# The 7x7 offset convolution of a deformable layer: from even and odd columns to even and odd rows and columns, with its weights read from DRAM piece by piece

## The chip, the core and the metric

The kernel runs on one core of a Trainium2 chip. A core has a matrix engine (TensorE, PE in the profile), three engines for elementwise work (VectorE, called DVE; ScalarE, called ACT; GpSimd, called POOL), a sync engine (SP) that here only issues DMAs, an on-chip memory with 128 partitions (SBUF), and an accumulator memory that the matrix engine writes (PSUM). The engines run independent instruction streams, each in its own order, and wait for each other by semaphores. The metric is the device time of one launch in microseconds (us), less is better. The kernel takes 9018.82 us (median of three runs, 9018.04 to 9021.72). The profiled execution took 9017.3 us, of which 9015.5 us are the span from its first to its last instruction.

## What is computed

The input is 8 samples of 384 channels of 32x32 pixels in float32. Four residual layers follow each other, each on a group-normalised input. The change touches the second, the deformable layer. It splits the channels into three groups of 128 with kernel sizes 3, 5 and 7, and for each group does this:

```python
def deform_block(x, ow, ob, dw, pw, pb, K):
    pad = K // 2
    offsets = conv2d(x, ow, ob, pad)          # 128 channels -> 2*K*K
    out = deform_depthwise(x, offsets, dw, K, pad)
    return conv2d(out, pw, pb, 0)

c3, c5, c7 = jnp.split(x, 3, axis=1)
out = jnp.concatenate([deform_block(c3, ..., 3), deform_block(c5, ..., 5), deform_block(c7, ..., 7)], axis=1)
return out * se_weight(out, fc1_w, fc2_w)
```

`deform_depthwise` samples the input bilinearly at K*K shifted positions per pixel, weighs each by the channel's depthwise weight and sums. The change is about `conv2d(x, ow, ob, 3)` for K = 7: 128 input channels, 98 output channels, 49 taps.

## The kernel before

The deformable layer is `deform_fast`. For each sample it handles the groups g = 0, 1, 2 (K = 3, 5, 7). The taps of a group are gathered into octets of eight taps that share the partitions, and one octet of a single tap; an octet is split into four parts (two for the single tap). One part of one octet is a **unit**. A sample has 6 + 14 + 26 = 46 units, numbered through all samples; `first[b, g]` is the first unit of group g of sample b, and t0 stands below for `first[b, 0]`.

In each unit VectorE makes weighted input cells (`fxk`, `weigh`, line 1640) and products of two hat functions (`fsm`, `product`, line 1657), and TensorE multiplies them into five PSUM banks (`wacc`, `products`, line 1694: 32 recorded instructions, 8 for a part of the single tap, two for each float32 matmul). The hats come from ScalarE (`hats_x`, lines 1600 and 1605, into `fhx`; `hats_y`, lines 1617 and 1622, into `fhy`), two buffers each, made from sampling positions (`fpyx`) that a DMA reads back from DRAM and spreads over the partitions.

The order of work on PE, DVE and ACT is written out by hand (`tc.manual_schedule`): a loop over unit numbers u, here called **slots**. In slot u the code emits, in this order: the load of positions due (`loads`), what was put in places act0, pe0 and dve0 of the slot, TensorE's products of unit u alternating with VectorE's work for unit u + 1, the hats due, and places act1, dve1 and pe1. `put(slot, place, fn)` fills the places. SP's order is not written out; its queue takes the DMAs of all these steps.

The three offset convolutions of sample b are spread through the slots of the sample before. The 3x3 one (`conv`, line 1317) is put whole at t0 - 13, the 5x5 one in six pieces at t0 - 12 to t0 - 7. The 7x7 one (`fir`, line 1279) is put in 14 pieces at t0 to t0 + 13. All use one PSUM bank (tag "conv", one buffer).

The 7x7 convolution already uses a trick along x: even and odd output columns share work. `fir_sum` (line 1265, at t0 - 1) adds even and odd columns of the input into `xs`; three accumulations (parts) over half-width images with 3, 4 and 4 combined column weights replace two with seven each. With seven rows these are 77 matmuls for 98 outputs, each over up to 512 positions (32 rows by 16 columns). `fir_take` evacuates a part: ScalarE for the shared sum (line 1288), VectorE adding it for the even and the odd columns (line 1293). The 11 combined columns of each of the seven rows are made once by `fir_weights` (DMAs on ACT's queue, six subtractions on POOL, line 1196) and stay in SBUF as `fow7`: 77 x 98 floats, 30.2 KB in each partition. `fir_end` then checks the range, adds the grid and writes the positions to DRAM at t0 + 14.

When a group's last unit is done, `sums_act` (ScalarE, line 1396) copies part of `wacc` and `sums` (VectorE, line 1401) adds the rest, both at the first slot of the next group; TensorE cannot start the next group before both are done, since `wacc` has one buffer.

Of the kernel before, what the change touches and what calls it, by code (L numbers as in the profile page):

```python
# [60 lines left out]
    ((0, 1), (-1, 0), (1, 2)),  # L61
    ((0, 6), (-2, 3), (-1, 7), (1, 9)),
    ((0, 5), (-1, 10), (1, 8), (2, 4)),
)
HXN, HYN, SMN = 1856, 1792, 832
# [34 lines left out]
class Net:  # L100
# [956 lines left out]
    def deform_fast(self, src, dst):  # L1057
        tc, nc, ins = self.tc, self.nc, self.ins
        with ExitStack() as ctx:
            wp = ctx.enter_context(tc.tile_pool(name="w1f", bufs=1))  # L1060
            self.q1 = ctx.enter_context(tc.tile_pool(name="q1", bufs=1))
            self.q2 = ctx.enter_context(tc.tile_pool(name="q2", bufs=2))
            self.mm = ctx.enter_context(tc.tile_pool(name="mm1", bufs=2, space=PSUM))
            self.win_acc = ctx.enter_context(tc.tile_pool(name="win_acc", bufs=1, space=PSUM))

            self.xn0 = self.q1.tile([P, G, L], F32, name="fxn")
            nc.sync.dma_start(out=self.xn0, in_=src(0))
            self.f = {}
            for g, K in enumerate(KS):
# [3 lines left out]
                ow = wp.tile([P, K * NFIR if n == 1 else K2, rows if n == 1 else st], F32, name=f"fow{K}")  # L1073
# [5 lines left out]
                if n == 1:  # L1079
                    self.fir_weights(ow, ins[f"ow{K}"])  # L1080
                else:
                    queue.dma_start(out=ow[:, :, :rows], in_=ins[f"ow{K}"])
# [44 lines left out]
            for u, (b, g, j, h) in enumerate(units):  # L1127
                if h == 0:
                    one = self.parts(g, j) == 2
                    loads[u - (4 if one else 5)] = b, g, j  # L1130
                    for t, fn, k in (
                        ((-2, self.hats_x, 0), (-2, self.hats_y, 0), (-1, self.hats_y, 1))
                        if one
                        else ((-3, self.hats_x, 0), (-2, self.hats_y, 0), (-1, self.hats_y, 1), (0, self.hats_x, 1))
                    ):
                        hats.setdefault(u + t, []).append((fn, b, g, j, k))
# [12 lines left out]
            with tc.manual_schedule(engines=engines):  # L1149
                for u in range(min(slots), max(slots) + 1):  # L1150
# [16 lines left out]
                    for fn, *args in sorted(hats.get(u, ()), key=lambda h: h[0] == self.hats_y):  # L1167
# [21 lines left out]
    def fir_weights(self, ow, src):  # L1189
        nc = self.nc  # L1190
        w = ow.rearrange("p (y k) o -> p y k o", k=NFIR)
        v = src.rearrange("p (y x) o -> p y x o", x=7)
        for k, x in enumerate((1, 3, 5, 0, 6, 2, 4)):
            nc.scalar.dma_start(out=w[:, :, k, :], in_=v[:, :, x, :])
        for d, i, j in ((7, 5, 0), (8, 6, 2), (9, 4, 2), (10, 3, 0), (5, 5, 1), (6, 6, 1)):
            nc.gpsimd.tensor_tensor(w[:, :, d, :], w[:, :, i, :], w[:, :, j, :], ALU.subtract)


    def block_steps(self, b, g, first, put, weights, src, dst):
# [62 lines left out]
        def fir_sum():  # L1262
            xs = s["xs"] = self.q1.tile([P, H, W // 2], F32, name="fxs", tag="fxs")
            x4 = xg().rearrange("p (h i e) -> p h i e", e=2, i=W // 2)
            nc.vector.tensor_tensor(xs, x4[:, :, :, 0], x4[:, :, :, 1], ALU.add)


        def fir(part, t0, t1):
            if t0 == 0:
                s["ps"] = self.mm.tile([P, HL], F32, name="ps_off", tag="conv", bufs=1)  # L1270
            x4 = xg().rearrange("p (h i e) -> p h i e", e=2, i=W // 2)
            x3 = (s["xs"], x4[:, :, :, 1], x4[:, :, :, 0])[part]
            o = s["ps"][:used].rearrange("p (h i) -> p h i", i=W // 2)
            work = [(dy, d, k) for dy in (0, -3, -2, -1, 1, 2, 3) for d, k in FIR[part]]
            for t in range(t0, t1):
                dy, d, k = work[t]
                ya, yb = max(0, -dy), min(H, H - dy)
                xa, xb = max(0, -d), min(W // 2, W // 2 - d)
                nc.tensor.matmul(  # L1279
                    o[:, ya:yb, xa:xb], ow[:, (dy + pad) * NFIR + k, :],  # L1280
                    x3[:, ya + dy : yb + dy, xa + d : xb + d], start=(t == 0), stop=(t == len(work) - 1),
                )

        def fir_take(part):
            ps = s["ps"][:used]
            if part == 0:
                s["fs"] = self.q1.tile([P, HL], F32, name="ffs", tag="fxs")
                nc.scalar.activation(s["fs"][:used], ps, AF.Identity, bias=ob[:used])
                return
            if part == 1:  # L1290
                s["pos"] = self.q1.tile([P, cols], F32, name="fpos", tag="fpos")
            pos = s["pos"][:used].rearrange("p (i e) -> p i e", e=2)[:, :, part - 1]
            nc.vector.tensor_tensor(pos, ps, s["fs"][:used], ALU.add)
# [170 lines left out]

        if g == 0:
            t = s0 - self.units_of(G - 1)
# [11 lines left out]
            put(t + 13, "pe1", conv, 0, 0, K2)  # L1478
            put(t + 14, "dve0", offsets, 0)
        elif g == 1:  # L1480
            t = first[b, 0] - 12
            for i in range(6):
                put(t + i, "pe1", conv, 0, K2 * i // 6, K2 * (i + 1) // 6)
            put(t + 6, "dve0", offsets, 0)
        else:
            t = first[b, 0]
            put(t - 1, "dve1", fir_sum)
            k = 0
            for part, pieces in enumerate((4, 5, 5)):
                nw = K * len(FIR[part])  # L1490
                for i in range(pieces):
                    where = "pe0" if t + k in (first[b, 0], first[b, 1]) else "pe1"
                    put(t + k, where, fir, part, nw * i // pieces, nw * (i + 1) // pieces)
                    k += 1
                put(t + k, "dve0" if part else "act0", fir_take, part)
# [130 lines left out]
    def unit_dve(self, b, g, j, part):  # L1626
# [9 lines left out]
        def weigh(k):  # L1636
            t = self.q2.tile([P, 8, P], F32, name="fxk", tag="fxk", bufs=3)
# [399 lines left out]
```

## Time and profile before

| | |
|---|---|
| median of three runs | 9018.82 us |
| profiled execution, whole | 9017.3 us |
| its span | 9015.5 us |
| busy PE / DVE / ACT / POOL over the span | 7552.9 / 7509.5 / 5808.8 / 5548.2 us |
| mean granted TensorE clock | 0.911 of full |
| first wacc matmul of samples 3 and 4 | 3855.5 and 4179.7 us |
| matmuls of line 1279, recorded instructions | 1232 |
| matmuls of line 1317, recorded instructions | 1376 |
| matmuls of line 1694, recorded instructions | 10624 |

Busy times are unions of an engine's instructions. The profile records two PE instructions for each float32 matmul (1232 is 8 samples x 77 x 2), with overlapping durations, so that only the union or the distance between starts says what a matmul costs. The deformable layer lies between about 2795 us (its first DMAs) and 5450 us; in the forty slices of the busy table these are slices 13 to 24, where POOL is idle. After its start one sample follows the other every 324.2 us. The numbers for a stretch of time are read from the busy times by windows, those for a line from its group of instructions in a window.

### The profile page before, as it was taken

To read this page: it belongs to the slowest core of one execution; us is meant where nothing else is said; L and a number is where in the kernel's file an instruction comes from. 1 tells how busy PE (TensorE), PEld (TensorE's weight loads), DVE (VectorE), ACT (ScalarE), POOL (GpSimd) and SP (SyncE) were. 2 spreads that over 40 slices of the span, in tenths; PEclk is the share of its full clock that TensorE was granted. 3 is DMA by queue.
4 is the path that set the end of the run, shared out by engine and by line. 5 is a ranking of instruction groups with operands and counts; after the bars stand their busy time and mean duration, and the time that the engine had idled before them with its cause. 6 is when DMAs were issued, how large, how long until landed. Compare 5 with 4: busy or idle time off the path is not lost. (4 is left out here: it accounts for less than half of the span.)

```text
span 9015.5 us, 90034 instructions
## 1 busy us (share of the span) xinstructions
PE 7552.9 (84%) x29176; PEld 3742.1 (42%) x29176; DVE 7509.5 (83%) x8421; ACT 5808.8 (64%) x9437; POOL 5548.2 (62%) x3362
## 2 busy tenths in 40 slices
PE   7888888888886999989899895688888888888876
PEld 2232232232223767767766772233333333333333
DVE  6999999999994878877877885888888989888872
ACT  6777777777773555555655564676767777776740
POOL 6999999999993000000000003898998989899954
PEclk8899899899887999999999997899998999899988
DMA  4545545545544253253443433466666656666646
GB/s 128 124 122 123 124 122 123 124 122 122 124 120 111 73 129 93 78 131 93 102 107 102 109 90 99 121 148 150 150 155 160 147 145 147 154 147 153 159 140 114
DMA packets 786426, 1122.96 MB, mean 125 GB/s; under 512 B 269266, under 2 KB 420978, under 8 KB 752152
## 3 DMA queue, kind: packets, MB, share of 16 engines
q1 hardware_dynamic: 724548, 1107.05, 50.1%
q10 hardware_dynamic: 61396, 10.06, 0.7%
q8 instruction: 232, 3.80, 0.2%
q14 instruction: 250, 2.05, 0.1%
HBM read 933.97 MB, written 182.91 MB: 124 GB/s over the span
## 5 line engine op out<-in xcount | busy, mean ns | idle before, releaser
L531 POOL TENSOR_TENSOR db<-dub,bc 128x1024 f32<-128x1024 f32 x1536 | 3605.4, 2356 | 372.1 <-DVE hs L543 171.4
L523 ACT ACTIVATE da<-dtb,vec 128x512 f32<-128x512 f32 x3072 | 2122.4, 691 | 604.0 <-DVE hs L556 404.8
L543 DVE TENSOR_TENSOR_SCAN da<-da,db 128x1024 f32<-128x1024 f32 x960 | 2193.2, 2285 | 128.1 <-ACT da L523 89.0
L464 POOL TENSOR_TENSOR dt<-dt,sp_e 128x512 f32<-128x512 f32 x96 | 122.4, 1275 | 2715.5 <-DMA bc<-bcd 2711.3
L1694 PE MATMUL wacc<-fsm,fxk 128*128 128x195 f32 (+21 forms) x10624 | 1584.2, 306 | 190.0 <-DVE fsm L1657 88.7
L1694 PEld LDWEIGHTS wacc<-fsm,fxk 128*128 128x128 f32 x10624 | 1469.9, 194 | 366.6 <-DVE fsm L1657 180.6
L543 DVE TENSOR_TENSOR_SCAN hs<-da,db 128x1024 f32<-128x1024 f32 x576 | 1315.3, 2283 | 195.7 <-POOL db L516 80.6
L554 POOL TENSOR_TENSOR hs<-hs,bc 128x1024 f32<-128x1024 f32 x576 | 1356.8, 2356 | 33.2 <-ACT st L549 33.2
L1657 DVE TENSOR_TENSOR fsm<-fhy,fhx 128x143 f32<-128x143 f32 (+40 forms) x3280 | 1088.4, 396 | 295.3 <-PE wacc L1694 283.3
L556 DVE TENSOR_TENSOR hs<-da,bc 128x1024 f32<-128x1024 f32 x960 | 1175.6, 1225 | 124.6 <-PE y L566 75.5
L566 PE MATMUL y<-hs,cols 128*32 128x512 f32 x6144 | 971.3, 644 | 290.8 <-POOL hs L554 267.2
L1640 DVE TENSOR_TENSOR fxk<-fxt,fwk 128x1024 f32<-128x1024 f32 (+1 forms) x688 | 814.3, 1184 | 35.1 <-PE wacc L1694 28.3
L1617 ACT ACTIVATE fhy<-fpyx,cell 128x416 f32<-128x416 f32 (+10 forms) x832 | 422.8, 580 | 523.6 <-DVE fsm L1657 523.2
L566 PEld LDWEIGHTS y<-hs,cols 128*32 128x32 f32 x6144 | 190.1, 113 | 1006.3 <-issue 484.1
L643 PE MATMUL ps_m<-hid,wm 128*128 128x512 f32 x1152 | 550.7, 633 | 62.0 <-ACT hid L638 27.9
L1600 ACT ACTIVATE fhx<-fpyx,cell 128x416 f32<-128x416 f32 (+10 forms) x664 | 372.0, 629 | 347.8 <-DVE fsm L1657 347.8
L624 PE MATMUL ps_h<-t,wm 128*128 128x512 f32 x1152 | 529.4, 603 | 42.4 <-DVE sp_e L456 26.0
L356 PE MATMUL ps_in<-xn,winr 128*128 128x512 f32 x576 | 328.1, 716 | 173.9 <-ACT xn L345 125.6
L643 PEld LDWEIGHTS ps_m<-hid,wm 128*128 128x128 f32 x1152 | 226.7, 202 | 395.2 <-issue 282.3
L1279 PE MATMUL ps_off<-fxn,fow 128*98 128x465 f32 (+10 forms) x896 | 385.8, 579 | 0.0
L624 PEld LDWEIGHTS ps_h<-t,wm 128*128 128x128 f32 x1152 | 215.4, 192 | 361.3 <-issue 272.9
L575 PE MATMUL ps_z<-xn,winr 128*128 128x512 f32 x576 | 303.0, 674 | 47.7 <-DVE sp_e L456 47.7
(215 smaller groups left out, 9675.8 us busy)
## 6 DMA issues: line engine op xcount, KB each, us to landing
dtb<-dtd SPq DMA_DIRECT2D x768, 256.0 KB
dub<-dtd SPq DMA_DIRECT2D x768, 256.0 KB
fpyx<-fposd SPq DMA_DIRECT2D x104, 1024.0 KB
fxt<-fxd SPq DMA_DIRECT2D x96, 1024.0 KB
wm<-in_w SPq DMA_DIRECT2D x96, 768.0 KB
bc<-bcd SPq DMA_DIRECT2D x256, 256.0 KB
x<-x SPq DMA_DIRECT2D x71, 768.0 KB
dtd<-dt SPq DMA_DIRECT2D x192, 256.0 KB
```

The lines of the kernel that those rows point to most:

```text
L523: nc.scalar.activation(da[:, i, :], s["dtb", j][:, k, :], AF.Exp, scale=na[:, j, n + i : n + i + 1])
L531: nc.gpsimd.tensor_tensor(db, du, s["bc"][p][:, 0], ALU.mult)
L543: nc.vector.tensor_tensor_scan(h1, da1, db1, 0.0, ALU.mult, ALU.add)
L554: nc.gpsimd.tensor_tensor(s["hs", m], s["hs", m], c, ALU.mult)
L556: nc.vector.tensor_tensor(hs_tile(s, m), s["da", m], c, ALU.mult)
L566: nc.tensor.matmul(s["y"][k * IP : (k + 1) * IP, :], sel, s["hs", p * NSUB + k][:, i, :], start=mlp and p == 0 and i == 0, stop=p == NQP - ...
L624: nc.tensor.matmul(ps, s["w1", q][:, k, f * P : (f + 1) * P], s["t"][:, k, :], start=(k == 0), stop=(k == G - 1))
L643: nc.tensor.matmul(ps, s["w2", q][:, f, o * P : (o + 1) * P], s["hid", q][:, f, :], start=(f == 0), stop=(f == 3))
L1617: nc.scalar.activation(hy[:, at : at + (yb - ya) * W], s["pyx", j][:, 0, ya * W : yb * W], AF.Abs, bias=bias)
L1640: nc.vector.tensor_tensor(t[:, :n], x, wk[:, j : j + 1, :].to_broadcast([P, n, P]), ALU.mult)
L1657: nc.vector.tensor_tensor(self.sub(sm, at, [(r * w, n), (w, r), (1, w)]), self.sub(hy, hy_at[by] + xa, [(r * W, n), (W, r), (1, w)]), self ...
L1694: nc.tensor.matmul(a[:, ya - 4 * o : yb - 4 * o, xa:xb], k, self.sub(sm, sm_at[by], [(w, yb - ya), (1, w)]), start=o not in s["open"], sto ...
```

## The change

The 7x7 convolution is split along y in the same way as along x. Its input becomes nine images of 16 x 16: sums and single phases of rows times sums and single phases of columns. The 11 x 11 = 121 combined weights serve 121 matmuls of up to 256 positions. They are worked out in five accumulations (`FIR_PH`), two blocks of them side by side in the PSUM bank in four of the five, and in 3 + 2 + 3 + 4 + 4 = 16 pieces (`FIR_PC`).

The combined weights no longer stay in SBUF. `fir_weights` makes them once in a temporary pool (47.4 KB per partition), with nine loads on ACT's queue, 18 subtractions on POOL and nine stores on ACT's queue to a DRAM tile `fwd` (121 x 98 x 128 floats, 6.07 MB). The temporary pool is closed before the pool `q2` is opened, so that the tiles of `q2` take its place. In each sample every piece loads its own six to eight weights into one of four buffers, three slots ahead.

The pieces move: 3x3 from one piece at t0 - 13 to three at t0 - 17 to t0 - 15; 5x5 from six at t0 - 12 on to nine at t0 - 14 to t0 - 6; 7x7 from 14 at t0 on to 16 at t0 - 5 to t0 + 10, with `fir_sum` at t0 - 6 and `fir_end` at t0 + 11. The load and the normalisation of a sample's input move four slots ahead, from t0 - 25 to t0 - 14 to t0 - 29 to t0 - 18. The positions of a single-tap octet are loaded five slots ahead instead of four and its `hats_x` made three slots ahead instead of two; in a slot with both kinds of hats, `hats_y` comes first. `fxk` has four buffers instead of three, `fsm` seven instead of five.

```diff
+FIR = (((0, 0), (-1, 1), (1, 2)), ((0, 3), (-2, 4), (-1, 5), (1, 6)), ((0, 7), (-1, 8), (1, 9), (2, 10)))
+FIR_PH = (((0, 0), (0, 1)), ((0, 2),), ((1, 0), (2, 0)), ((1, 1), (2, 1)), ((1, 2), (2, 2)))
+FIR_PC = (3, 2, 3, 4, 4)
...
+            self.fwd = self.dram.tile([P, NFIR * NFIR, 2 * 49], F32, name="fwd", bufs=1)
+            with tc.tile_pool(name="fw", bufs=1) as fw:
+                self.fir_weights(fw.tile([P, NFIR, NFIR, 2 * 49], F32, name="firw"), ins["owf"])
             self.q2 = ctx.enter_context(tc.tile_pool(name="q2", bufs=2))
...
-                    loads[u - (4 if one else 5)] = b, g, j
+                    loads[u - 5] = b, g, j
...
-                        ((-2, self.hats_x, 0), (-2, self.hats_y, 0), (-1, self.hats_y, 1))
+                        ((-3, self.hats_x, 0), (-2, self.hats_y, 0), (-1, self.hats_y, 1))
...
-                    for fn, *args in sorted(hats.get(u, ()), key=lambda h: h[0] == self.hats_y):
+                    for fn, *args in sorted(hats.get(u, ()), key=lambda h: h[0] == self.hats_x):
...
-        for k, x in enumerate((1, 3, 5, 0, 6, 2, 4)):
-            nc.scalar.dma_start(out=w[:, :, k, :], in_=v[:, :, x, :])
-        for d, i, j in ((7, 5, 0), (8, 6, 2), (9, 4, 2), (10, 3, 0), (5, 5, 1), (6, 6, 1)):
-            nc.gpsimd.tensor_tensor(w[:, :, d, :], w[:, :, i, :], w[:, :, j, :], ALU.subtract)
+        at = ((slice(0, 5), slice(0, 5)), (slice(7, 8), slice(5, 6)), (slice(10, 11), slice(6, 7)))
+        for y, ys in at:
+            for x, xs in at:
+                nc.scalar.dma_start(out=w[:, y, x, :], in_=src[:, ys, xs, :])
+        diffs = ((5, 7, 1), (7, 7, 0), (9, 3, 2), (3, 3, 0), (6, 10, 2), (8, 4, 1))
+        for d, i, j in diffs:
+            for y in (slice(0, 5), slice(7, 11, 3)):
+                nc.gpsimd.tensor_tensor(w[:, y, d, :], w[:, y, i, :], w[:, y, j, :], ALU.subtract)
+        for d, i, j in diffs:
+            nc.gpsimd.tensor_tensor(w[:, d], w[:, i], w[:, j], ALU.subtract)
...
+            nc.scalar.dma_start(out=o, in_=w[:, r0:r1, c0:c1, :].rearrange("p r c o -> p r (c o)"))
...
         def fir_sum():
...
+            nc.vector.tensor_tensor(xs, x[:, :, :, 0], x[:, :, :, 1], ALU.add)
...
+            nc.vector.tensor_tensor(xr, x[:, :, 0], x[:, :, 1], ALU.add)
...
+            nc.vector.tensor_tensor(xss, xr[:, :, 0::2], xr[:, :, 1::2], ALU.add)
...
+        def fir_load(i):
+            k, _, piece = pieces[i]
+            t = s["fw", i] = self.q2.tile([P, FIR_W, used], F32, name="fw", tag="fw", bufs=4)
+            nc.sync.dma_start(out=t[:, : len(piece)], in_=self.fwd[:, k : k + len(piece)])
...
+                nc.tensor.matmul(
+                    o[:, ya:yb, xa:xb], s["fw", i][:, k, :],
+                    fir_src(r, c)[:, ya + dy : yb + dy, xa + dx : xb + dx], start=start, stop=stop,
+                )
...
-            put(t + 13, "pe1", conv, 0, 0, K2)
-            put(t + 14, "dve0", offsets, 0)
+            for i in range(3):
+                put(t0 - 17 + i, "pe1", conv, 0, 3 * i, 3 * i + 3)
+            put(t0 - 14, "dve0", offsets, 0)
...
+            for i in range(9):
+                put(t0 - 14 + i, "pe1", conv, 0, K2 * i // 9, K2 * (i + 1) // 9)
+            put(t0 - 5, "dve0", offsets, 0)
...
+            put(t0 - 6, "dve1", fir_sum)
+            t = t0 - 5
             k = 0
-            for part, pieces in enumerate((4, 5, 5)):
...
+            for ph, n_pc in enumerate(FIR_PC):
+                for _ in range(n_pc):
+                    put(t + k - 3, "dve0", fir_load, k)
+                    put(t + k, "pe0" if t + k in (t0, first[b, 1]) else "pe1", fir, k)
                     k += 1
-                put(t + k, "dve0" if part else "act0", fir_take, part)
+                put(t + k, "dve0" if ph > 1 else "act0", fir_take, ph)
             put(t + k, "dve0", fir_end)
...
-            t = self.q2.tile([P, 8, P], F32, name="fxk", tag="fxk", bufs=3)
+            t = self.q2.tile([P, 8, P], F32, name="fxk", tag="fxk", bufs=4)
...
-            sm = self.q2.tile([P, SMN], F32, name="fsm", tag="fsm", bufs=5)
+            sm = self.q2.tile([P, SMN], F32, name="fsm", tag="fsm", bufs=7)
```

The new `fir_take` evacuates five accumulations. The first two (ScalarE, three copies of 256 values) go to `fs`; the third is combined with them by three VectorE additions of 2 x 256 values; the fourth and the fifth each take two VectorE additions of 256 values into `fpos`. Four of these takes must be done before the next accumulation's first piece may start, since the PSUM bank has one buffer.

## The prediction

> **What bounds the kernel.** I read the page's busy slices first, to see where the layer lies and which engine is full there, then one sample by stretches, then the groups of the convolution's line, then the timeline at the one long gap. The layer is slices 13 to 24:
>
> ```profile
> PE   7888888888886999989899895688888888888876
> DVE  6999999999994878877877885888888989888872
> ```
>
> TensorE is at eight or nine tenths and VectorE at seven or eight. A period (324.2 us, sample 3 to 4) by stretches; columns are the stretch, its length, busy time (and count) of PE, weight loads, DVE, ACT and POOL, clock, DMA share, GB/s:
>
> ```profile
> 3848.87:3964.18 115.31, 112.84 (x535) 71.35 (x535) 73.03 (x159) 63.68 (x98) 0.00 (x0) 1.00 0.47 121
> 3964.18:3993.73 29.55, 26.14 (x185) 24.98 (x183) 29.25 (x62) 13.84 (x19) 0.00 (x0) 0.88 0.55 148
> 3993.73:4005.43 11.70, 2.04 (x17) 1.94 (x17) 5.23 (x14) 10.65 (x18) 0.00 (x0) 0.80 1.01 258
> 4005.43:4085.00 79.57, 71.64 (x431) 64.47 (x431) 77.17 (x166) 51.91 (x71) 0.00 (x0) 0.94 0.30 71
> 4085.00:4139.10 54.10, 54.10 (x376) 39.90 (x374) 41.21 (x92) 30.33 (x40) 0.00 (x0) 1.00 0.14 41
> 4139.10:4173.06 33.96, 30.84 (x202) 28.46 (x201) 33.59 (x70) 16.20 (x25) 0.00 (x0) 1.00 0.51 120
> ```
>
> The first stretch holds the 7x7 convolution (slots t0 to t0 + 13), the fifth the 3x3 and 5x5 ones: there TensorE has no gap and VectorE idles. In the second, fourth and sixth no convolution runs and VectorE is full. The third is a gap: K = 5 ends, K = 7 begins, and PE waits 9.65 us behind ScalarE's hats and copies. So **a matmul saved counts only in stretches one and five**, and matmuls moved to stretch six count in full, as its PE slack is 3 us. The convolution:
>
> ```profile
> L1279 PE MATMUL ps_off<-fxn,fow 128*98 128x480 f32 (+10 forms) x112 | 48.2, 579 | 0.0
> L1279 PE MATMUL ps_off<-fxs,fow 128*98 128x480 f32 (+6 forms) x43 | 17.7, 557 | 2.6 <-DVE fxs L1265 2.6
> ```
>
> `fxs` is read with adjacent elements, `fxn` with every second. The mean tile is 464.4 positions for `fxs` (30.29 rows after clipping by 15.33 columns) and 454.3 for `fxn` (30.29 by 15). Busy time per instruction, 17.7 / 43 = 412 ns and 48.2 / 112 = 430 ns, gives **0.886 ns and 0.947 ns a position**.
>
> **Matmuls, step by step.** Before: 21 contiguous and 56 stride-2 matmuls of two instructions, 42 x 0.412 + 112 x 0.430 = 65.5 us a sample. After: clipped sums over the nine images give 7,636 contiguous positions (33 matmuls) and 19,920 stride-2 ones (88), against 9,752 and 25,440. Cost 2 x (7,636 x 0.886 + 19,920 x 0.947) = 51.3 us. **Saved: 14.2 us of TensorE a sample.** Two bounds on the price. Smaller tiles: the wacc group's instructions (L1694) take 198.7 / 1328 = 150 ns on tiles of 143 positions in the mean, 1.04 ns a position with all small ones in it; that is the upper end for the new mean of 228 (57.3 us), and the lower end is the old price. Strided rows: [...] by the row stride-2 costs 7% more and it is 51.3. I take the row. New images also skip every second line of rows, which no row shows: if that doubles the stride's surcharge, 2 x 19,920 x 0.061 = 2.4 us is lost[...].
>
> **By stretch after the change**, at 51.3 / 121 = 0.424 us a matmul:
> - Stretch six gains pieces 0 to 4 (33 matmuls, 14.0 us) and becomes TensorE's: 30.84 + 14.0 = 44.8 us (before 33.96).
> - Group boundary at t0. Before, PE waited 1.3 + 2.47 us. Now piece 5 opens accumulation three at the head of the slot and needs the take of accumulation two, behind ScalarE's hats and `sums_act`. In the trace these end at 3853.2; TensorE would be free at 3847.5 + 3.2 = 3850.7. With the 0.4 us copy the wait is 2.9 us, VectorE's `sums` beside piece 5.
> - Slots t0 to t0 + 10: PE's work outside the convolution in stretch one is 112.84 - 65.1 = 47.7, of which slots t0 + 11 to t0 + 13 hold 11.8. So 35.9 + 88 x 0.424 = 73.2. ScalarE has 12.5 us of work at the K = 3 to 5 boundary where PE will have 9.7: plus 3.
> - Slots t0 + 11 to t0 + 13 lose their pieces and fall to VectorE: 15.2 us of its work there (before 25.4).
> - Stretches two to four: 120.8 us. Two more `fsm` buffers let VectorE enter them two products ahead (0.6 + 0.6 us each with its share of `fxk`): minus 2.5. At the gap, `hats_y` first changes nothing: `sums_act` still waits for both hats, which start at VectorE's last product (3994.54).
> - Convolutions 3x3 and 5x5: 54.1 us as before; spreading them over slots t0 - 17 to t0 - 6 (4060.6 to 4143.6) uses PE's slack there, 2.0 of 83.0 us: minus 1.5.
>
> Sum 44.8 + 2.9 + 76.2 + 15.2 + 118.3 + 52.6 = 310.0, saving 14.2 a sample. That it equals the matmul saving is chance: more waits appear, some go.
>
> **Other engines.** VectorE gains 1.1 us in `fir_sum` (0.7 + 0.7 + 0.4 for 0.7) and 2.4 in the takes (three of 0.69, four of about 0.42 by the 0.40 us products, for two of 0.69), most of it where it idles 42 us; without that cover it would cost 3.5 a sample. ScalarE's 0.7 us more is inside its waits.
>
> **DMA.** Each sample adds 16 loads and 6.07 MB on SP's queue, 27 us at the 225 GB/s seen when the DMAs are full. From 3830 to 3900 they are 0.86 busy (211 GB/s): cells and positions, 1 MB each, 4.6 us. Slots t0 - 5 to t0 + 8 hold 16 MB; with 4.9 MB more that is 93 us of transfer in about 103. So it fits, barely. A load is issued three slots ahead (some 20 us) and waits in SP's order for the buffer of four pieces before, freed one slot earlier; behind it wait positions and cells. [...] by the row, cells go out as buffers free (3837.6, 3838.3, 3839.4, 3844.9), and the fourth overlaps less. [...] I take **1 us**. Saving 13.2 x 8 samples = 106 us.
>
> **Start of the layer, once.** ACT's queue gets 11 more DMAs at 0.55 us, before the normalisation's square that waited for that queue until 2833.9: 6 us. POOL subtracts 23.5 us (six each of 490, 196 and 1,078 values at 1,524 ns per 686, for 9.1): from 2808.3 to 2832, so the stores do not wait much longer than ACT would. They take 28 us to about 2865, where the DMAs are 0.27 busy, and hold the memory under `q2`; the first positions, needed at 2873.8, come after. Piece 0 follows the 5x5 convolution (end 2867.7 + 6). Ends -5 and +30; I take **+6**.
>
> **Forecast**: 9017.3 - 106 + 6 = **8917 us**; against the median, 1.5 above the profiled execution, it would be 8919, a difference that the range swallows. Its own range is 8885 to 8945.
>
> **Rivals.**
> - *Half is lost* to waits in the shorter stretch one (ScalarE at each boundary, five takes on one bank instead of three, DMA at 90%): 6 us a sample more, 8965. For it: ScalarE's 12.5 us at the boundary, the full DMAs. Against: VectorE is further ahead there.
> - *Balance closes stalls too*: VectorE waited 36.2 us a sample for PE in `fsm`, and PE 10.3 for VectorE. If the deeper buffers remove half the 10 us gap and 4 of those 10.3, 8 x 9 more goes: 8845. Against: the gap is ScalarE's.
> - *Slower*: the weights come late. Loads of eight pieces (t0 - 1 to t0 + 6) sit behind the cells; if each stops TensorE for half a 1 MB transfer, 2.3 us, that is 18.4 a sample against 14.2 saved: 9017.3 + 34 + 6 = 9057. It decides from 0.9 us a piece (14.2 / 16). For it: DMAs at 1.0 in two runs of ten us there. Against: three slots of lead.
>
> Chances: forecast 0.52, half lost 0.22, balance 0.19, slower 0.07. 0.2% is 18 us, about what a measurement of this kernel can tell from no change: faster by that 0.92, within it 0.03 (the tail of the half-lost case), slower 0.05. The range for eight in ten runs from 8840 to 8970.
>
> **What would show it.** The convolution's group at about 51 us a sample, 0.42 us a matmul, stride-2 tiles dearer; the period at 310; PE without gaps from t0 - 5 to t0 + 10 but 3 us at t0 and t0 + 6; slots t0 + 11 on with VectorE full; the gap before K = 7 still near 10 us; few or no PE waits ended by a DMA of the piece weights. It would be wrong if those waits are there by the dozen, or if the first wacc matmul comes later than 2920.

## The result and the profile after

The changed kernel takes **8857.13 us** (median of four runs, 8852.23 to 8860.34) against 9018.67 us before: ratio 0.982, 95% interval 0.9803 to 0.9837. It is 161.5 us faster; 8917 us was forecast. The profiled execution took 8859.41 us, its span is 8857.3 us.

The busy tenths, in 40 equal slices of the span:

```profile
PE   7888888888884899999999975788888888888886
DVE  6999999999995788988898886888898988888872
```

The layer lies in slices 13 to 24 as before. After worse slices 13 and 14 (4 and 8 for 6 and 9) TensorE stands at nine tenths up to slice 23, where before it fell to eight three times, and VectorE fills up too. The gain is in the steady part of the layer and its start is dearer.

For both kernels I cut one sample's period at the slots at which groups and convolutions begin: slots 0 to 10 from t0, 11 to 19, 20 to 28, 29 to 40, 41 to 45. Busy time by these windows, before (columns as in the forecast: stretch, its length, busy time and count of PE, weight loads, DVE, ACT and POOL, clock, DMA share, GB/s):

```profile
3855.52:3938.80 83.28, 83.28 (x394) 52.82 (x395) 55.62 (x121) 46.88 (x73) 0.00 (x0) 1.00 0.53 138
3938.80:4005.43 66.63, 53.57 (x332) 43.88 (x330) 49.68 (x110) 34.71 (x52) 0.00 (x0) 0.91 0.47 127
4005.43:4060.61 55.18, 49.24 (x280) 42.97 (x281) 52.78 (x111) 33.53 (x44) 0.00 (x0) 0.92 0.35 83
4060.61:4143.64 83.03, 81.04 (x559) 65.92 (x557) 69.92 (x155) 48.91 (x67) 0.00 (x0) 1.00 0.16 42
4143.64:4179.71 36.07, 30.48 (x180) 25.49 (x179) 31.47 (x67) 22.58 (x36) 0.00 (x0) 1.00 0.65 147
```

and after:

```profile
3813.64:3884.16 70.52, 70.52 (x445) 60.80 (x445) 52.28 (x117) 46.70 (x72) 0.00 (x0) 1.00 0.82 211
3884.16:3941.84 57.68, 42.22 (x298) 40.39 (x297) 53.28 (x119) 33.61 (x50) 0.00 (x0) 0.85 0.57 161
3941.84:3990.66 48.82, 46.05 (x280) 40.50 (x280) 48.79 (x106) 35.64 (x51) 0.00 (x0) 0.97 0.38 83
3990.66:4072.62 81.96, 81.92 (x557) 64.29 (x557) 74.05 (x161) 51.75 (x69) 0.00 (x0) 1.00 0.15 40
4072.62:4113.61 40.99, 40.53 (x251) 36.95 (x251) 32.35 (x67) 19.62 (x33) 0.00 (x0) 1.00 0.80 193
```

A period falls from 324.2 to 300.0 us, 24.2 a sample. TensorE's busy time falls by 16.4 (297.6 to 281.2), its idle time by 7.9 (26.6 to 18.7), and VectorE's idle time from 64.7 to 39.2 at the same work. The first two stretches lose 12.8 and 9.0 us, the third 6.4 although it holds no convolution in either kernel, the fourth 1.1; the last, which takes pieces in (17.8 us of 7x7 matmuls for 4.2), grows by only 4.9. TensorE is now full in the first, fourth and fifth, and VectorE in the third.

The groups of the period after (line, engine, operation, tiles, count, busy us and mean ns, idle before and what ended it):

```profile
L1759 PE MATMUL wacc<-fsm,fxk 128*128 128x143 f32 (+31 forms) x1328 | 196.0, 306 | 18.3 <-ACT fhy L1682 9.7 <-DVE fsm L1722 8.3
L1722 DVE TENSOR_TENSOR fsm<-fhy,fhx 128x132 f32<-128x132 f32 (+35 forms) x410 | 135.4, 399 | 7.3 <-PE wacc L1759 7.2
L1320 PE MATMUL ps_off<-fxn,fw 128*98 128x210 f32 (+5 forms) x128 | 27.3, 366 | 0.0
L1320 PE MATMUL ps_off<-fxq,fw 128*98 128x240 f32 (+4 forms) x48 | 10.8, 374 | 0.0
L1320 PE MATMUL ps_off<-fxs,fw 128*98 128x225 f32 (+4 forms) x50 | 10.4, 359 | 0.5 <-ACT ffs L1335 0.5
L1320 PE MATMUL ps_off<-fxss,fw 128*98 128x240 f32 (+2 forms) x18 | 3.9, 362 | 0.0
```

The four rows of line 1320 are the new 7x7 convolution: 52.4 us with the overlaps of the rows counted twice, 51.8 as a union (65.3 before), against the forecast of 51.3. Its one wait is 0.5 us, for a copy; no wait of TensorE in the period is ended by a DMA of the piece weights. The wait of 9.7 us for ScalarE's `fhy`, ahead of K = 7, is what it was. VectorE's `fsm` waited 36.2 us for TensorE before and waits 7.2 now.

At the start of the layer the loss shows on ACT's queue (start, length, queue or engine, operation; in brackets the idle time before it):

```profile
2796.27 15.74 ACTq L1197 DMA_DIRECT2D firw<-in_owf  x9
2812.15 31.01 ACTq L1209 DMA_DIRECT2D fwd<-firw  x9
...
2855.51 0.17 ACT L178 ACTIVATE gn_dm<-gn_ps 128x3 f32<-128x3 f32 x1 [87.41 <-DMA pwb<-in_pwb]
```

The nine stores hold the queue from 2812.15 to 2843.2: until 2831.2 POOL's subtractions go on (from 2808.2), and it takes 12 us more until the last store is issued; what holds it there is not shown. The normalisation's square stands behind them and behind the setup's small loads, at 2855.51 instead of 2833.93, 21.6 us later. The first wacc matmul comes at 2918.1 instead of 2886.7, 31.4 us later; the other 9.8 us lie between the two, where 82 recorded 7x7 instructions now stand ahead of the first product (10 before). So: start +31.4, seven periods -170.1 (2265.5 to 2095.4), last sample to the end of the layer -23.0, sum -161.7, by which the layer's last instruction comes earlier.

### The profile page after: what moved, and what is told of

Its sections match the earlier page's. It is cut to its first block, busy times and chain, and to the rows that moved or that the text cites. A ratio compares the mean times of both kernels' runs of the same rounds, so it can differ in the third digit from the quotient of the medians.

```text
span 8857.3 us, 91757 instructions
## 1 busy us (share of the span) xinstructions
PE 7449.8 (84%) x29880; PEld 3853.8 (44%) x29880; DVE 7519.8 (85%) x8477; ACT 5818.6 (66%) x9453; POOL 5565.4 (63%) x3374
## 5 line engine op out<-in xcount | busy, mean ns | idle before, releaser
L1687 ACT ACTIVATE fhy<-fhy,cols 128x1184 f32<-128x1184 f32 (+8 forms) x208 | 307.6, 1479 | 6.8
```

## The experiments

Two things were to be explained: why a sample gains 24.2 us and not 13.2, and why the start costs 31 and not 6. The first four runs take the change's parts out again, the fifth puts one of them alone into the kernel before, and the rest try what is left at the start, at the gap and in the place of the pieces. Each time is a median of four runs, that of e5 of twelve; the kernel before took 9017.06 us beside the first four, 9019.18 beside the next four and 9017.87 beside the last three.

**e1_bufs**: the kernel after with the buffers of before.

```diff
-            t = self.q2.tile([P, 8, P], F32, name="fxk", tag="fxk", bufs=4)
+            t = self.q2.tile([P, 8, P], F32, name="fxk", tag="fxk", bufs=3)
...
-            sm = self.q2.tile([P, SMN], F32, name="fsm", tag="fsm", bufs=7)
+            sm = self.q2.tile([P, SMN], F32, name="fsm", tag="fsm", bufs=5)
```

> The changed kernel with the old number of buffers, three for fxk and five for fsm, all else as changed. Theory A (the 10 us a sample that the forecast did not see come from VectorE running further ahead through the deeper buffers): the period goes from 300.0 back to 308 to 311 us, VectorE's waits for TensorE in fsm rise from 7 to over 25 us a sample, whole time 8920 to 8945 us. Theory B (they come from the hats made and loaded earlier, hats_y first): period 300 to 302, time 8857 to 8873. Theory C (they come from the 3x3 and 5x5 pieces spread out): the same as B here.

Measured: 8863.37 us (ratio 0.983, 0.9813 to 0.9846), period 300.4 to 300.7 from the third sample on; the first two periods are each some 3 us longer than in the kernel after. The group of `fsm` in one period of this kernel:

```profile
L1722 DVE TENSOR_TENSOR fsm<-fhy,fhx 128x300 f32<-128x300 f32 (+34 forms) x410 | 135.5, 390 | 21.0 <-PE wacc L1759 21.0
```

VectorE's wait for TensorE triples, from 7.2 to 21.0 us, and the steady period grows by some 0.5. The wait is that of an engine with time to spare. The deeper buffers are worth some 0.5 us in a steady sample, not the 2.5 of the forecast.

**e2_hats**: the kernel after with the old times and order of the hats.

```diff
-                    loads[u - 5] = b, g, j
+                    loads[u - (4 if one else 5)] = b, g, j
...
-                        ((-3, self.hats_x, 0), (-2, self.hats_y, 0), (-1, self.hats_y, 1))
+                        ((-2, self.hats_x, 0), (-2, self.hats_y, 0), (-1, self.hats_y, 1))
...
-                    for fn, *args in sorted(hats.get(u, ()), key=lambda h: h[0] == self.hats_x):
+                    for fn, *args in sorted(hats.get(u, ()), key=lambda h: h[0] == self.hats_y):
```

> The changed kernel with the old times of a single-tap octet (positions four slots ahead, hats_x two slots ahead) and the old order of hats (hats_x first), all else as changed. Theory A (deeper buffers): period 300 to 301 us, time within 10 us of 8857. Theory B (hats): period 306 to 310, ScalarE's hats again late at the three group boundaries, time 8905 to 8940. Theory C (spread pieces): as A here.

Measured: 8861.61 us (ratio 0.9826, 0.9809 to 0.9842), period 299.9. The hats' new places are worth nothing that can be seen, as forecast for the order at the gap.

**e3_conv**: the kernel after with the 3x3 and 5x5 convolutions in their old places.

```diff
-            for i in range(3):
-                put(t0 - 17 + i, "pe1", conv, 0, 3 * i, 3 * i + 3)
-            put(t0 - 14, "dve0", offsets, 0)
+            put(t0 - 13, "pe1", conv, 0, 0, K2)
+            put(t0 - 12, "dve0", offsets, 0)
...
-            for i in range(9):
-                put(t0 - 14 + i, "pe1", conv, 0, K2 * i // 9, K2 * (i + 1) // 9)
-            put(t0 - 5, "dve0", offsets, 0)
+            for i in range(6):
+                put(t0 - 12 + i, "pe1", conv, 0, K2 * i // 6, K2 * (i + 1) // 6)
+            put(t0 - 6, "dve0", offsets, 0)
```

> The changed kernel with the 3x3 convolution whole at t0 - 13 and the 5x5 one in six pieces from t0 - 12 on, as before the change; the 7x7 one stays at t0 - 5 on. Theory A (deeper buffers): TensorE's full stretch is cut in two, so VectorE's lead is spent in the middle: period 301 to 303 us, time 8865 to 8885. Theory B (hats): period 300. Theory C (spread pieces): period 307 to 310, time 8910 to 8940.

Measured: 8884.2 us (ratio 0.9853, 0.9837 to 0.987), period 303.6. Slots 29 to 40 take 84.9 us for 82.0, slots 41 to 45 0.7 more. Spreading is worth 3.6 us a sample, more than twice the forecast's 1.5, but not enough for the whole excess.

**e4_split_only**: the edits of e1, e2 and e3 together, and the 7x7 pieces where they had been. What is left of the change is the split with its weights in pieces, and the earlier load and normalisation.

```diff
-            put(t0 - 6, "dve1", fir_sum)
-            t = t0 - 5
+            put(t0 - 2, "dve1", fir_sum)
+            t = t0 - 1
```

> The split along y with its weights read by pieces and nothing else: old buffers, old hats, old places of the 3x3 and 5x5 pieces, and the 7x7 pieces at t0 - 1 to t0 + 14. All theories: TensorE's work falls by 13.5 us a sample, and where VectorE was idle already nothing more is won. By the forecast's account of the matmuls alone the period is 310 to 312 us, the start 10 to 25 us late, time 8925 to 8945. If the period is 303 or less, the extra gain lies in the split itself and none of A, B and C holds.

Measured: 8887.42 us (ratio 0.9855, 0.9839 to 0.9872), first wacc 2903.5, period 305.4. The busy times by the same stretches of this kernel:

```profile
3823.14:3891.76 68.62, 68.62 (x434) 59.31 (x435) 54.90 (x119) 45.56 (x73) 0.00 (x0) 1.00 0.84 222
3891.76:3956.18 64.42, 51.92 (x361) 48.66 (x360) 54.52 (x121) 36.47 (x53) 0.00 (x0) 0.90 0.61 173
3956.18:4007.55 51.37, 49.21 (x281) 44.02 (x281) 48.96 (x106) 35.62 (x51) 0.00 (x0) 0.90 0.35 80
4007.55:4092.48 84.93, 83.56 (x556) 67.73 (x557) 71.31 (x156) 46.80 (x61) 0.00 (x0) 0.98 0.15 41
4092.48:4128.52 36.04, 32.24 (x199) 28.45 (x197) 32.46 (x69) 22.58 (x36) 0.00 (x0) 1.00 0.68 157
```

The first stretch falls by 14.7 us, exactly what its convolution loses (46.4 to 31.7). TensorE has no gap in it, though the boundary K = 3 to 5 and the DMAs at 0.84 lie there: the wait charged at this boundary does not exist. (The other one, at t0, is not tested by this run, since its third accumulation does not open there.) The last stretch is as long as before: its two pieces (6.0 us) stand where one of 4.2 us stood, and the 1.8 us more lie in TensorE's old idle time (5.6). And slots 20 to 28 are 3.8 us shorter with no convolution at all.

**e5_before_norm**: that last piece alone, in the kernel before: load and normalisation four slots earlier.

```diff
-            t = s0 - self.units_of(G - 1)
+            t = s0 - self.units_of(G - 1) - 4
...
-            put(t + 13, "pe1", conv, 0, 0, K2)
-            put(t + 14, "dve0", offsets, 0)
+            put(t + 17, "pe1", conv, 0, 0, K2)
+            put(t + 18, "dve0", offsets, 0)
```

> The kernel before the change with one edit: the load and normalisation of a sample four slots earlier (tied to t0 - 30), the 3x3 convolution staying at t0 - 13. Theory D (part of the gain comes from VectorE's statistics moving out of its full stretch into the gap at the start of K = 7, where it idles): period 324.2 to 319.5 to 321.5, slots t0 + 20 to t0 + 28 from 55.2 to 50 to 52 us, time 8982 to 9000. Theory E (this move is worth nothing; the gain there comes with the shorter 7x7 pieces): period 323.5 to 324.5, time within 8 us of 9017.

Measured: 9014.85 us (12 runs, 9009.55 to 9019.14; ratio 0.9995, 0.9987 to 1.0004), period 324.3: no difference. Of its stretches, the first, third and fourth:

```profile
3848.84:3933.77 84.93, 84.93 (x394) 54.08 (x395) 55.61 (x121) 47.10 (x73) 0.00 (x0) 0.98 0.56 137
...
4000.39:4052.15 51.76, 48.84 (x281) 42.69 (x281) 48.98 (x106) 35.62 (x51) 0.00 (x0) 0.91 0.22 55
4052.15:4137.08 84.93, 82.74 (x556) 66.21 (x557) 71.35 (x156) 46.81 (x61) 0.00 (x0) 1.00 0.16 41
```

Slots 20 to 28 lose 3.4 us, because VectorE's work there falls from 52.78 to 48.98; slots 29 to 40 give 1.9 back and the first stretch 1.6. So most of the 3.8 us of e4's third stretch are this move. That a VectorE stretch gets shorter was left out of the forecast; alone it is worth nothing. In e4 the fourth stretch has the same 84.93, and the spreading of the convolutions (e3) brings it down to 82.0: what each of the two is worth depends on the other.

**e6_stores_sp**: the kernel after with the nine stores on SP's queue.

```diff
-            nc.scalar.dma_start(out=o, in_=w[:, r0:r1, c0:c1, :].rearrange("p r c o -> p r (c o)"))
+            nc.sync.dma_start(out=o, in_=w[:, r0:r1, c0:c1, :].rearrange("p r c o -> p r (c o)"))
```

> The changed kernel with one edit: the nine stores of the combined weights are issued from SP's queue instead of ACT's. If the late start (first wacc matmul 2918 instead of 2887 us) comes from ACT's queue standing 31 us behind the stores, the normalisation's square falls from 2855 to 2825 to 2840 us, the first wacc matmul to 2890 to 2905, the time to 8833 to 8848. If it comes from POOL's subtractions and the DRAM round trip themselves, the first wacc matmul stays at 2910 or later and the time within 8 us of 8857.

Measured: 8841.8 us (ratio 0.9807, 0.979 to 0.9823), first wacc 2903.8, periods unchanged. The square of the normalisation now comes at 2825.45, earlier than in the kernel before, but the wait has moved. TensorE's timeline of this kernel at the 5x5 convolution:

```profile
2853.87 22.02 PE L1382 MATMUL ps_off<-fxn,fow 128*64 128x512 f32 x100 [14.54 <-DMA fow<-in_ow]
```

The weights of the 5x5 convolution now stand behind the stores on SP's queue: the loads of `fow` are issued after the last store, whose turn comes at 2839.2. Of the 30 us by which the square comes earlier 16 are given back.

**e7_early_sums**: the gap ahead of K = 7. At this boundary `sums_act` stands in ScalarE's order behind the hats for the slots to come; here it comes first, and the hats of the single tap's second part and of the next octet come behind it.

```diff
-                        ((-3, self.hats_x, 0), (-2, self.hats_y, 0), (-1, self.hats_y, 1))
+                        ((-3, self.hats_x, 0), (-2, self.hats_y, 0))
                         if one
+                        else ((-2, self.hats_y, 0), (-1, self.hats_y, 1), (0, self.hats_x, 1))
+                        if self.parts(g, units[u - 1][2]) == 2
...
+                    if one:
+                        early.setdefault(u, []).append((self.hats_y, b, g, j, 1))
+                    elif self.parts(g, units[u - 1][2]) == 2:
+                        early.setdefault(u - 2, []).append((self.hats_x, b, g, j, 0))
...
+                    for fn, *args in early.get(u, ()):
+                        fn(*args)
```

> The changed kernel with one edit: at the first slot of a group, sums_act goes ahead of two groups of hats in ScalarE's order (hats_y of the single tap's second part and hats_x of the next octet are emitted after place act0). If the 10 us gap at the start of K = 7 is the order of ScalarE's queue, TensorE waits 3 to 6 us there instead of 9.7, period 295 to 298, time 8825 to 8845. If it is ScalarE's amount of work there, the wait only moves to the next unit: period 299 to 301, time within 10 us of 8857.

Measured: 8847.51 us (ratio 0.981, 0.9794 to 0.9827), period 298.6 to 299.7. Slots 11 to 19 lose 4.2 us, as the gap gets shorter (5.53 us for 9.7); slots 20 to 28 take 3.3 of them back. There TensorE's busy time rises from 46.05 to 49.60 us for the same matmuls, while its clock falls from 0.97 to 0.86. The stretches of 4 us around the gap of the kernel after (PE busy time and count are the third and fourth figure, the clock is the third from the end):

```profile
3932.00:3936.00 4.00, 0.18 (x2) 0.04 (x1) 3.73 (x7) 3.97 (x7) 0.00 (x0) 0.84 1.06 229
3936.00:3940.00 4.00, 0.00 (x0) 0.00 (x0) 0.24 (x1) 3.97 (x7) 0.00 (x0) 0.50 1.04 225
3940.00:3944.00 4.00, 2.16 (x4) 1.52 (x5) 3.93 (x9) 3.29 (x6) 0.00 (x0) 0.50 0.98 207
3944.00:3948.00 4.00, 4.00 (x13) 2.35 (x12) 4.00 (x12) 3.65 (x5) 0.00 (x0) 0.88 1.03 223
3948.00:3952.00 4.00, 4.00 (x25) 2.77 (x23) 4.00 (x9) 2.63 (x5) 0.00 (x0) 1.00 0.69 150
```

and of e7:

```profile
3933.00:3937.00 4.00, 4.00 (x11) 2.17 (x10) 2.47 (x6) 3.97 (x6) 0.00 (x0) 0.75 1.00 225
3937.00:3941.00 4.00, 2.53 (x8) 1.12 (x6) 3.40 (x10) 3.97 (x6) 0.00 (x0) 1.00 1.01 221
3941.00:3945.00 4.00, 3.17 (x15) 3.17 (x16) 4.00 (x9) 3.97 (x8) 0.00 (x0) 0.60 0.51 115
3945.00:3949.00 4.00, 4.00 (x17) 4.00 (x18) 3.32 (x7) 1.41 (x2) 0.00 (x0) 0.50 0.82 201
3949.00:3953.00 4.00, 4.00 (x18) 3.98 (x18) 3.96 (x8) 3.97 (x5) 0.00 (x0) 0.62 0.30 61
```

In the kernel after, the clock is at 0.50 in the gap and some 3 us beyond it, and at 1.00 from 3945 to the end of the stretch. In e7 it comes back too, and then dips a second time (0.60, 0.50 and 0.62) for some 10 us with matmuls in all of them: 17 or 18 in 4 us at 0.50 and 0.62, where the next row of e7 (3953 to 3957, clock 1.00) has 29 and the last of the kernel after 25. TensorE's timeline of e7 has the shorter gap and, behind it, the stop that lies ahead of this dip:

```profile
3930.87 6.94 PE L1767 MATMUL wacc<-fsm,fxk 128*128 128x288 f32 x16 [5.53 <-DVE fdsb L1474]
3937.65 1.88 PE L1480 MATMUL ps_pw<-fdsb,pwt 128*128 128x512 f32 x4
3941.83 4.00 PE L151 MATMUL gn_ps<-gn_mv,gmat 128*128 128x2 f32 x18 [2.30 <-ACT fog L1486]
3945.69 12.75 PE L1767 MATMUL wacc<-fsm,fxk 128*128 128x88 f32 x64
```

This stop is a new wait of 2.30 us: ScalarE, now busy with the hats that were put behind `sums_act` (3.97 of each 4 us), makes `fog`, the output of the last convolution, later than TensorE wants it. So the stretch becomes TensorE's; VectorE idles 3.0 us in it where it had idled 0.0.

**e8_fir_t0**: the kernel after with the 7x7 pieces at t0 - 1 to t0 + 14 (the edit of e4), and the positions of the single tap loaded one slot later.

> The changed kernel with the 16 pieces of the 7x7 convolution at t0 - 1 to t0 + 14 instead of t0 - 5 to t0 + 10 (and the single tap's positions four slots ahead, which these slots need). The slots t0 - 5 to t0 - 2 lose their pieces and fall to VectorE, t0 + 11 to t0 + 14 get them. If it only matters that every piece lies beside units where TensorE is full or has slack, 300 to 302 us a period. If the pieces at the end of K = 7 fill the wait at the group boundary t0, 303 to 306, time 8880 to 8905.

Measured: 8844.04 us (ratio 0.9805, 0.9789 to 0.9821), first wacc 2904.2, period 298.7. Moving the pieces ahead to t0 - 5 thus gained nothing: it costs 1.3 us in a steady sample. It also costs 13.9 us at the start, where 28 recorded 7x7 instructions stand ahead of the first product here and 82 in the kernel after; the first and the last sample take 9 us of all this back. Behind t0 + 10 pieces fill TensorE's stops, and the clock is 1.00 in that stretch, for 0.86 in the kernel after. The slots from t0 + 11 on, of this kernel and of the kernel after:

```profile
3870.00:3906.00 36.00, 33.83 (x238) 31.07 (x237) 29.53 (x64) 16.35 (x23) 0.00 (x0) 1.00 0.29 90
```

```profile
3884.00:3920.00 36.00, 31.35 (x218) 30.67 (x216) 35.54 (x78) 17.25 (x25) 0.00 (x0) 0.86 0.29 97
```

**e9_setup_stores**: e6, with the layer's setup emitted ahead of the combined weights, so that the 3x3 and 5x5 weights stand ahead of the stores on SP's queue.

```diff
-            self.fwd = self.dram.tile([P, NFIR * NFIR, 2 * 49], F32, name="fwd", bufs=1)
-            with tc.tile_pool(name="fw", bufs=1) as fw:
-                self.fir_weights(fw.tile([P, NFIR, NFIR, 2 * 49], F32, name="firw"), ins["owf"])
...
             nc.gpsimd.memset(self.far, -1.0)
+            self.fwd = self.dram.tile([P, NFIR * NFIR, 2 * 49], F32, name="fwd", bufs=1)
+            with tc.tile_pool(name="fw", bufs=1) as fw:
+                self.fir_weights(fw.tile([P, NFIR, NFIR, 2 * 49], F32, name="firw"), ins["owf"])
```

> The kernel after, with the nine stores of the combined weights on SP's queue and the layer's setup (its small loads, the 3x3 and 5x5 weights among them) emitted ahead of the combined weights. If what the start still costs is the 3x3 and 5x5 weights behind the stores on SP's queue (14.5 us of wait in e6_stores_sp): first wacc matmul at 2887 to 2893, time 8825 to 8832, periods unchanged at 300. If the start is bounded by the subtractions and by the piece weights that can't be read before the stores land (about 2865): first wacc stays at 2900 to 2905, time 8838 to 8845.

Measured: 8827.92 us (ratio 0.9792, 0.9776 to 0.9809), first wacc 2888.4, periods 299.9. TensorE's timeline of this kernel:

```profile
2840.09 20.11 PE L1382 MATMUL ps_off<-fxn,fow 128*64 128x512 f32 x100 [1.72 <-DVE far L1403]
2862.64 4.71 PE L1320 MATMUL ps_off<-fxss,fw 128*98 128x256 f32 x14 [2.44 <-DVE far L1403]
```

The wait for `fow` is gone and the first 7x7 piece follows 2.44 us behind the 5x5 convolution, at 2862.6. The nine loads, 18 subtractions, nine stores and the 6 MB written are all still there. So the order of the two queues, not the amount of work on them, cost 29.7 us. The first wacc matmul is nearly back where it was before the change (2886.7), but the 82 recorded 7x7 instructions ahead of it are not free: from the square to that matmul 62.6 us pass (52.8 before), and the square comes 8.2 us earlier than before (2825.78), which makes up for most of it.

**e10_setup_fir_t0**: e9 and e8 together.

> e9_setup_stores and the 7x7 pieces at t0 - 1 to t0 + 14, as in e8_fir_t0. If the two gains are at different places (the start, and the slots after t0) they add: 8844.0 less what the setup takes away in e9 (28 us at most): 8816 to 8822, period 298.7, first wacc 2880 to 2886. If the pieces at t0 - 1 had already taken away the same wait at the start, nothing adds: 8835 to 8845.

Measured: 8818.43 us (ratio 0.978, 0.9764 to 0.9796), first wacc 2874.7, period 298.6. Against the sum of the two gains (13.1 and 29.2 us, 8814.8) 3.6 us are missing: the first period, 305.0 us, is 4.9 longer than in e8, and the steady ones are the same. So the two add but for that.

**e11_all**: e10 and the early sums of e7.

> e10_setup_fir_t0 and the early sums of e7_early_sums. If the gap before K = 7 is worth what it was there (12 us in all): 8804 to 8812, period 297 to 298. If ScalarE's or VectorE's amount in the slots after the gap sets the pace, as in e7_early_sums, and the later pieces have already used PE's slack there: no gain, 8816 to 8822.

Measured: **8795.12 us** (8790.27 to 8796.87; ratio 0.9754, 0.9738 to 0.977), periods 295.0 to 296.9 after the first: lower than either expectation. The second and third stretch of a period of this kernel:

```profile
3834.50:3894.81 60.31, 50.73 (x361) 46.05 (x360) 54.00 (x121) 29.85 (x45) 0.00 (x0) 0.98 0.56 165
3894.81:3946.89 52.08, 49.58 (x280) 45.51 (x281) 49.05 (x106) 40.55 (x59) 0.00 (x0) 0.86 0.41 93
```

The third is as long as in e7 (52.1), with the clock at the same 0.86; the second, with pieces in the stops ahead of the gap, has a clock of 0.98 and loses 4.1 us against e10's 64.4; slots 41 to 45 lose another 1.6. This is the fastest version that was run, 62 us below the changed kernel. The early sums bring 23 us here and 10 without the later pieces. The trace shows one reason: at t0 ScalarE's copies of `wacc` begin 4.6 us behind TensorE's last product in e10, and at once in e11, while in the kernel after they begin at once anyway. TensorE's wait of 1.44 us there is gone. The rest of the difference is not settled.

## Why the prediction was right or wrong

**Right**: the direction, a time inside the stated range, the price of the matmuls (51.3 us forecast, 51.8 measured), that they count only where TensorE has no gap, that stride-2 tiles are dearer (0.948 and 0.978 ns a position for 0.904 and 0.922), that no piece of weights comes late, that the gap before K = 7 keeps its size (9.7), and that the hats' order changes nothing. The slower case did not come: the DMAs run at 0.80 to 0.82 in the crowded stretches and no wait of TensorE ends with them, so the 1 us a sample charged for them, which was my estimate, is also gone.

**Wrong in size**, by stretches, with the forecast's own terms put on the same borders (44.8 + 2.9 + 76.2, less 4.5 that lie before slot 41; 15.2 + 118.3, less 24.4 behind slot 28; 24.4 + 52.6 + 4.5):

| slots | forecast | measured | what was mis-sized |
|---|---|---|---|
| 41 to 45 and 0 to 10 | 119.4 | 111.5 | two waits charged at boundaries, 2.9 + 3 us: 0.5 measured. wacc in slots 41 to 45: 23.4 us, charged as before at 25.5 |
| 11 to 28 | 109.1 | 106.5 | buffers charged as 2.5 gained: 0.5. The earlier normalisation, not priced: 3.4 gained |
| 29 to 40 | 81.5 | 82.0 | 1.5 gained: 1.0 measured, as the normalisation's 1.9 against the spreading's 2.9 |
| period | 310.0 | 300.0 | |

- *The step that failed most* is "PE without gaps from t0 - 5 to t0 + 10 but 3 us at t0 and t0 + 6". It kept ScalarE as far behind TensorE as in the old trace. ScalarE's copies of `wacc` at t0, before:

```profile
3852.16 1.05 ACT L1396 COPY fdsb<-wacc 128x512 f32<-128x512 f32 x2
```

  after, and in e8:

```profile
3807.53 1.07 ACT L1461 COPY fdsb<-wacc 128x512 f32<-128x512 f32 x2 [2.29 <-PE wacc L1759]
```

```profile
3798.24 1.05 ACT L1461 COPY fdsb<-wacc 128x512 f32<-128x512 f32 x2
```

  TensorE's last product ended at 3847.57, 3807.49 and 3793.64. So before the change the copies began 4.6 us behind it; in the kernel after ScalarE stands ready and waits for TensorE. The pieces moved into slots 41 to 45 give TensorE more to do there and VectorE nothing: its last `fsm` product of the sample ends 8.9 us before TensorE's last product starts, where it was 0.95. In e4 and e8, which have only two pieces there, it is 0.95 again and the copies are 4.6 us behind, so it is these pieces and not the shorter convolution. The hats' new places are not it (e2 has 8.9 too), nor the buffers, as e1 has 5.9 and its copies begin at once. At the boundary K = 3 to 5 the copies end 1.3 us behind TensorE's last product, and 6.7 us of pieces cover that.
- *The second* is stretch six: that the pieces "count in full" there, and its 30.84 us of PE taken as work. Pieces of 13.6 us more lengthen slots 41 to 45 by 4.9, since TensorE's idle time goes from 5.6 to 0.5 us and wacc gets cheaper. The trace's own groups show the same 160 instructions (25.50 us in slots 41 to 45 before, with 5.6 us idle) at 23.36 us when other matmuls lie between them:

```profile
4143.64:4179.71 36.07, 25.50 (x162) 23.01 (x161) 1.00 0.65 147
```

```profile
4072.62:4113.61 40.99, 23.36 (x160) 23.32 (x161) 1.00 0.80 193
```

  (The first fence is wacc alone in that stretch before, the second after; columns are PE and its weight loads, then clock and DMAs.) That the busy time of a stretch with stops is partly waiting is how I read these two rows; no run takes it apart further.
- *Buffers and spreading* were both given from waits in the trace. The wait that the buffers removed (21.0 to 7.2 us in e1) was not on the path; the spreading, whose cover was 2.0 us of idle time in the trace, was worth more than that, 3.6.
- *The start* went the other way: +31.4 us at the first wacc matmul where +6 was forecast, past the upper end of 30. The step "the stores do not wait much longer than ACT would" compared the end of the subtractions (2832, measured 2831.2) with an instruction that stood at 2833.9, and forgot that behind the stores stand eleven loads of the setup, and behind these the square: 21.6 us. For the 7x7 pieces ahead of the first product, 9.8 us, it has no term. e9 shows that the first part goes with another order, e8 that the second goes with later pieces.
- *The rivals*: the waits of the half-lost case are not there, as TensorE is full in slots 0 to 10. The case of closed stalls, 8845, was nearest in its number and wrong in its cause, since it had the deeper buffers halve the gap. The difference between 8917 and the profiled 8859.4 us, 57.6, adds up so: 11.0 us a sample more than forecast (10.0 in the period, 1.0 of DMA) are 88, less 25.4 at the start: 62.6. Most of the other 5 lies behind the layer, whose last instruction comes 161.7 us earlier while the span is 158.2 shorter. That two errors of opposite sign left 57.6 is chance.

**Open**: slots 11 to 28 gained 1.2 us more than the terms above explain (109.1 + 2.0 - 3.4 = 107.7 against 106.5), and what part of it the clock's dips have was not told apart. A version without the round trip of the weights through DRAM was not tried.

## What to carry to other kernels

A wait that the trace shows behind an engine is only to be kept in a forecast if that engine stays as far behind: work moved ahead of a boundary on one engine gives the others time to get ready for it (ScalarE's copies at t0 began 4.6 us behind TensorE before, and at once after). Busy time in a stretch with stops may be more than the work costs (25.5 us here for instructions that took 23.4 with other matmuls between them). For every instruction put on a DMA queue that waits, list what is behind it on the same queue down to the first instruction that the critical path needs: here that order alone cost 30 us, and the first repair moved the wait to the other queue. And look for stops of TensorE that other work can fill: some of those seen here were followed by a lower clock, in e7 one of 2.30 us by 0.50.

## What the hardware showed

- The price of a position by stride. From the groups of line 1320, busy time over count and mean size (230 positions for `fxs` and `fxq`, 225 for `fxn`, 235 for `fxss`, by the clipped sums): 0.904 ns for `fxs` (adjacent elements of every second row) and 0.948 for `fxn` (every second element of every second row); `fxss` (adjacent elements, all rows) 0.922 and `fxq` (every second element, all rows) 0.978. The stride costs 5 to 6%, and the skipped rows, for which the forecast kept 2.4 us a sample, cost nothing in these rows (0.904 with them for 0.922 without, 0.948 for 0.978). Tiles of half the size raised the price by 2% at most for the images that compare directly (0.886 to 0.904, 0.947 to 0.948).
- The granted clock was at 0.50 behind some stops of TensorE and stayed there for some microseconds of matmuls. In the kernel after it is at 0.50 from 2.6 us into the gap of 9.66 us to 3.1 us behind its end (3934.7 to 3945.0), in the kernel before from 5.0 us into the gap of 9.65 us to 5.6 us behind its end (4000.8 to 4011.0). In e7 it falls again behind a stop of 2.30 us that began 8.7 us after the gap of 5.53 us had ended, and behind a run of 18 matmuls of two columns (4.00 us in the timeline above). In e8 it falls to 0.64 (3946 to 3950) behind such a run of 2.17 us, with no stop in the 8 us ahead of it. What sets it off is not told apart by these runs.
